# The first attention unit's operands in three parts, two of them copied inside SBUF

## Chip, cores and metric

The kernel runs on one core of one Trainium2 chip. The metric is the device time of one execution in microseconds (us); a kernel's time is the median of its runs. The engines are TensorE (PE, with its weight loads listed as PEld), VectorE (DVE), ScalarE (ACT), GpSimd (POOL) and SyncE (SP). In this kernel SyncE issues every DMA.

## What is computed

The input x has 8 sequences of 1024 tokens with 256 channels. Three sublayers follow one another: half a feed-forward step, attention with relative positions (16 heads of 16 channels), and the same half feed-forward step again.

```python
x = x + 0.5 * tanh(layernorm(x) @ W1 @ W2 @ W3 + bias)
...
xn = layernorm(x) * ln_g + ln_b
q, k, v = xn @ Wq + bq, xn @ Wk + bk, xn @ Wv + bv        # 16 heads of 16
p = sinusoidal_pe(1024, 256) @ Wp
content = einsum('bihd,bjhd->bhij', q + u_bias, k)
pos = relative_shift(einsum('bihd,jhd->bhij', q + v_bias, p))
attn = softmax((content + pos) / 4)
x = x + einsum('bhij,bjhd->bihd', attn, v) @ Wo + bo
...
x = x + 0.5 * tanh(layernorm(x) @ W1 @ W2 @ W3 + bias)
```

## The kernel before

**Two stages.** In the first, the tokens go through in 8 tiles, I = 7 down to 0, each with 128 token positions of all 8 sequences. For each tile the kernel makes the first feed-forward step, the normalisation, and the projections to queries, keys and values. Values in 16-bit floats are held as a high and a low part (`hl` 0 and 1). The results leave for tensors in device memory: `k_d`, `qv_d` (queries in eight windows of 18 positions per tile), `c_d` (a bias row per key), `v_d` and `x1c_d`.

The second stage is attention. It is cut into 64 units: 16 heads times 4 groups of query positions (`rg`). A unit has 16 steps (`step(T)`), so there are 1024 steps. A step computes two score banks of 128 x 512 (`score_ops`), the row maxima (`block_max`, `row_max`), subtracts them and takes the exponential into `eT` (`soften`). After 16 steps `emit_av` multiplies `eT` by the values in `vt`.

**The order of the work** is written out by hand: each engine runs its instructions in the order of the program, and waits come from which buffers an instruction reads and writes. A buffer of a pool that is opened where an older pool lay waits for everything that used the old buffer there.

**The pass loop.** The loop at L660 runs I from 6 to -1. A pass makes the feed-forward step of tile I and the projections of tile I+1; the value products of tile I+2 (`value`, `late`) run at its start. Before its middle it stores V of tile I+2 (`store_v`, L685) and x1 of tile I+1 (`store_x1`, L686: eight additions on POOL, then one DMA). After the projections, `key_bias` (L716) makes the bias rows `cs`, and `store_qk` (L717) sends out keys, queries and bias rows of tile I+1: one DVE copy (`next_rows`) and ten DMAs. So the last pass, I = -1, projects tile 0 and stores V of tile 1 and x1 of tile 0 on the way. After the loop come the loads of the first unit (L721), the value products of tile 0 and its V store (L724).

**A unit's operands.** `UnitSet` holds them: `k` (keys, 8 chunks of the sequence, with bias rows at partitions 48, 49, 112 and 113), `qc` and `q` (queries in two layouts) and `pg` (positions). Two sets alternate. `load_q` loads queries from `qv_d` to a raw buffer (4 DMAs), `prep` yields 16 copies from the raw buffer into `qc` and `q`, and `load_k` loads keys and bias rows (6 DMAs). All three take all 8 chunks at once. For unit 0 the 16 copies are spread over POOL, DVE and ACT (L1064, L1065). A chunk is what one tile of the first stage makes: chunk i of `k` is tile i.

**Buffers around the seam.** `cvst[0]` and `cvst[1]` hold the projected queries of even and odd tiles and are the first buffers of pool `kp` (9,216 bytes per partition each); `kp` has 25,920 bytes. Behind it lies `pA`, with two buffers each of `xTb` (8,192), `cs` (2,048), `ks` (8,192) and `vs` (8,192). After `es.close()` (L860) the attention's pools lie there: `m2` (16,352 bytes: `many16`, `m0`, `m1`, `dg` and others) and behind it `ep` with the second raw buffer (4,608), `vt` (8,192) and `eT` (65,536).

Of the kernel before, what the change touches and what calls it, by code (L numbers as in the profile page):

```python
# [16 lines left out]
P = 128  # L17
NB = 8
# [4 lines left out]
NI = S // P  # L23
# [3 lines left out]
NW = 8  # L27
QP = 18
NTILE = 64 * H
MS = 16.0  # L30
UT = 16
# [11 lines left out]
def macaron_kernel(  # L43
# [23 lines left out]
    nc = tc.nc  # L67
# [8 lines left out]
    c_d = dram("c_d", (H, 2, NI, NB * P), F16)  # L76
# [50 lines left out]
    class UnitSet:  # L127
# [21 lines left out]
                w = 16 * (hl.stop - hl.start)  # L149
                yield slice(64 * n + p0, 64 * n + p0 + w), hl  # L150

        def load_q(self, u):
            rg, h = units[u]
            w = NB * QP * rg
            return [
                (
                    raws[u % 2][pr],
                    qv_d[h, hl].rearrange("t d i (e c) -> (t d) (i e) c", e=2)
                    [:, :, w : w + NB * QP],
                )  # L160
                for n in range(2) for pr, hl in self.rows(n, True)
            ]

        def prep(self, u):


            ops = []
            for n in range(2):
                pr = slice(64 * n, 64 * n + 48)
                raw = raws[u % 2][pr]  # L170
                src = raw.rearrange("p k (b t) -> p b t k", t=QP)
                for q in range(4):
                    ops.append(
                        (self.qc[pr, :, q, 16 * n : 16 * n + 16], src[:, 4 * n + q, 0:UT])
                    )
                src = raw.rearrange("p (k e) (b t) -> p e t k b", e=2, t=QP)[:, 1 - n]
                dst = self.q[pr].rearrange("p t (k b) e -> p e t k b", b=NB)[:, 1 - n]
                for t in (slice(0, 4), slice(4, 8), slice(8, 12), slice(12, 17)):
                    ops.append((dst[:, t], src[:, t]))
            return ops  # L180

        def load_p(self, u):
# [6 lines left out]
                for n in range(2) for pr, hl in self.rows(n, False)  # L189
            ]  # L190

        def load_k(self, u):
            rg, h = units[u]
            return [
                (
                    self.k[pr].rearrange("p i q r -> p i (q r)"),
                    k_d[h, hl].rearrange("t d i c -> (t d) i c")
                    [:, :, 4 * P * n : 4 * P * n + 4 * P],
                )
                for n in range(2) for pr, hl in self.rows(n, False)  # L200
            ] + [
                (
                    self.k[64 * n + 48 : 64 * n + 50].rearrange("p i q r -> p i (q r)"),
                    c_d[h, :, :, 4 * P * n : 4 * P * n + 4 * P],
                )
                for n in range(2)
            ]

    def load_all(pairs):
        for pair in pairs:  # L210
            nc.sync.dma_start(*pair)
# [4 lines left out]
    sets = [UnitSet(hp0, 0), UnitSet(hp1, 1)]  # L216
# [4 lines left out]
    raws = [raw(hp0, 0)]  # L221

    def copy16(dst, src):
        nc.gpsimd.tensor_scalar(dst, src, 1.0, 0.0, ALU.mult, ALU.add)  # L224
# [4 lines left out]
    if True:  # L229
# [5 lines left out]
        cvst = [  # L235
            kp.tile([P, 2, 2, NW, NB, QP], F16, tag=f"cv{i}", name=f"cv{i}") for i in range(2)
        ]
# [143 lines left out]
        def store_x1(I, xt):  # L381
            for b in range(NB):
                nc.gpsimd.tensor_tensor(xt[:, b, :], xt[:, b, :], cvec, ALU.add)
            nc.sync.dma_start(
                x1c_d[:, I * P : (I + 1) * P, :].rearrange("b p c -> p b c"), xt
            )
# [45 lines left out]
        def key_bias(ks, cs):  # L432


            ps = pst.tile([P, 512], F32, tag="t", name="kb")
            n = 0
            for m in range(2):
                for a, c in ((0, 0), (1, 0), (0, 1)):
                    for h in range(2):
                        mm(  # L440
                            ps[32 * h : 32 * h + 32], uv16[:, a, m, :],
                            ks[:, m, c, 4 * h : 4 * h + 4].rearrange("p b n -> p (b n)"),
                            start=n == 0, stop=n == 5, tile_position=(0, 32 * h),
                        )
                    n += 1
            nc.scalar.copy(cs[:, 0], ps[0:64])
            nc.vector.tensor_tensor(cs[:, 1], ps[0:64], cs[:, 0], ALU.subtract)
# [27 lines left out]
        def next_rows(I):  # L475
# [4 lines left out]
            else:  # L480
                nc.vector.memset(cv[:, :, NW - 1, :, 16], 0.0)

        def store_qk(I, cs, ks):
            next_rows(I)
            cv = cvst[I % 2]
            for m in range(2):
                for hl in range(2):
                    for dst, src in (
                        (k_d, ks[:, m, hl].rearrange("p b n -> p (b n)")),
                        (qv_d, cv[:, m, hl].rearrange("p w b n -> p (w b n)")),  # L490
                    ):
                        nc.sync.dma_start(dst[8 * m : 8 * m + 8, hl, :, I], src)
            for h in range(2):
                nc.sync.dma_start(
                    c_d[:, :, I, 512 * h : 512 * h + 512], cs[32 * h : 32 * h + H]
                )

        def store_v(I, vs):
            nc.sync.dma_start(
                v_d[:, :, I, :].rearrange("h p n -> p h n"),  # L500
                vs.rearrange("p h d b -> p h (d b)"),
            )
# [6 lines left out]
        xts = {NI - 1: load_x(NI - 1)}  # L509
# [149 lines left out]
        late = None  # L659
        for I in range(NI - 2, -2, -1):  # L660
            if I >= 0:
                xT, xt, so, sb = new_xT("a"), xts[I], sb, Stats("b", xts[I])
            if I >= 1:
                sa = Stats("a", xts[I - 1])
            for n in range(4):
                if late:
                    value(late[1], late[2], 2 * n)
                if I >= 0:
                    tr_group(xn, xT, n // 2, n % 2)
                if I >= 1:  # L670
                    sa.rows(2 * n, 2 * n + 2)
                if I == NI - 2 and n == 0:
                    so.again()
                if I == NI - 2 and n == 1:
                    so.both()
                    xm = so.apply("xm")
                    low(*los[2])
                    low(*los[3])
                    wes.close()
                    pA = es.enter_context(tc.tile_pool(name="pA", bufs=2))  # L680
                if n >= 2 and I >= 0:
                    ffn(xT, xt, n - 2)
                    sb.rows(2 * n - 4, 2 * n - 2)
            if late:
                store_v(late[0], late[2])  # L685
            store_x1(I + 1, xts.pop(I + 1))  # L686
            if I >= 2:
                xts[I - 2] = load_x(I - 2)
            if I >= 1:
                sa.ends()  # L690
                xn = sa.apply("xn")
            xTb = new_xT("b")
            for n in range(4):
                tr_group(xm, xTb, n // 2, n % 2)
                if n < 2 and I >= 0:
                    ffn(xT, xt, n + 2)
                    sb.rows(2 * n + 4, 2 * n + 6)
            cs = pA.tile([64, 2, 512], F16, tag="cs", name="cs")
            ks = pA.tile([P, 2, 2, NB, P], F16, tag="ks", name="ks")
            for n in range(4):  # L700
                q = query(xTb, cvst[(I + 1) % 2], n % 2, n // 2)
                k = key(xTb, ks, n % 2, n // 2)
                q()
                k()
                if I >= 0 and n == 0:
                    sb.ends()
                if I >= 0 and n == 1:
                    sb.again()
                if I >= 0 and n == 2:
                    sb.both()  # L710
                    xm = sb.apply("xm")
            if I == NI - 3:
                sets[0].clear()
            if I == NI - 4:
                sets[1].clear()
            key_bias(ks, cs)  # L716
            store_qk(I + 1, cs, ks)  # L717
            if I == 2:
                load_all(sets[0].load_p(0))
            late = (I + 1, xTb, pA.tile([P, H, DH, NB], F32, tag="vs", name="vs"))  # L720
    load_all(sets[0].load_q(0) + sets[0].load_k(0))  # L721
    for n in range(4):
        value(late[1], late[2], 2 * n)
    store_v(late[0], late[2])  # L724
# [336 lines left out]
                        pending.extend(post_ops(rg, b, m2, 1, psm, "r", {}))  # L1061

    nc.gpsimd.memset(vt[:, :, DH:, :], 1.0)
    for n, pair in enumerate(sets[0].prep(0)):  # L1064
        (copy16, nc.vector.tensor_copy, nc.scalar.copy)[n % 3](*pair)  # L1065
    load_all(load_v(0))
    for T in range(-2, NTILE - UT + 2):
        step(T)
# [51 lines left out]
    for n in range(4):  # L1120
        src = num[0][:, 2 * n : 2 * n + 2]
# [46 lines left out]
    def head(b):  # L1168
# [8 lines left out]
    ops = {  # L1177
        b: [f for f, _ in post_ops(rg, b, t3, NB, pm, "r", {"ps": ps[b], "xr": xr[:, b]})]
        for b in range(NB)
    }  # L1180
# [52 lines left out]
```

## Time and profile before

| what | us |
|---|---|
| median of 3 runs | 3067.61 (3058.85, 3067.61, 3070.53) |
| profiled execution | 3070.87 |
| its span, first to last instruction | 3069.2 |
| first stage, until TensorE's last value product ends | 282.55 |
| first score matmul | 302.02 |
| first maximum of a score bank (L933, DVE) | 303.14 |
| first exponential (L962, ACT) | 307.13 |

The page gives busy time by engine, the span in 40 slices, the chain of work that ended last, and groups of instructions by line. In a list in order of time, a row has the start, the duration, the engine, the source line, the operation, what it writes and reads with its shape, and how often it stands there in a row; in brackets is how long the engine was idle before it and what ended that. SPq is SyncE's queue: its rows are issues of DMAs, whose data land later. A row of a stretch gives the stretch, its length, the busy time and number of instructions of PE, PEld, DVE, ACT and POOL, the granted TensorE clock (1.00 is full speed), the share of the DMA engines' time and the GB/s moved.

### The profile page before, as it was taken

To read this page: it belongs to the slowest core of one execution; us is meant where nothing else is said; L and a number is where in the kernel's file an instruction comes from. 1 tells how busy PE (TensorE), PEld (TensorE's weight loads), DVE (VectorE), ACT (ScalarE), POOL (GpSimd) and SP (SyncE) were. 2 spreads that over 40 slices of the span, in tenths; PEclk is the share of its full clock that TensorE was granted. 3 is DMA by queue.
4 is the path that set the end of the run, shared out by engine and by line. 5 is a ranking of instruction groups with operands and counts; after the bars stand their busy time and mean duration, and the time that the engine had idled before them with its cause. 6 is when DMAs were issued, how large, how long until landed. Compare 5 with 4: busy or idle time off the path is not lost.

```text
span 3069.2 us, 157389 instructions
## 1 busy us (share of the span) xinstructions
PE 2939.8 (96%) x71212; PEld 2430.2 (79%) x71212; DVE 2264.0 (74%) x5001; ACT 1668.9 (54%) x3551; POOL 1000.7 (33%) x1498
## 2 busy tenths in 40 slices
PE   7997999999999999999999999999999999999986
PEld 4655888888888888888888888888888888888875
DVE  6885777777777877777777777787777787777766
ACT  3655555555555555555555555555555555555543
POOL 8873322222221332332221332332222333242204
PEclk8998999999999999999999999999999999999998
DMA  4556222222222322322222322322222232322222
GB/s 142 186 165 181 61 68 67 65 64 61 63 64 75 83 80 82 84 70 65 63 63 76 81 78 80 80 71 68 66 66 71 81 84 79 82 61 68 68 76 78
DMA packets 333397, 250.63 MB, mean 82 GB/s; under 512 B 118885, under 2 KB 317142, under 8 KB 332246
## 3 DMA queue, kind: packets, MB, share of 16 engines
q1 hardware_dynamic: 332726, 240.56, 28.1%
q8 instruction: 558, 9.14, 1.3%
q14 instruction: 113, 0.93, 0.1%
HBM read 177.44 MB, written 62.78 MB: 78 GB/s over the span
## 4 chain that ended last, share of the span: by engine, by line
PE 80%; DVE 5%; ACT 4%; DMA 2%; issue 1%; SPq 1%; POOL 0%; ACTq 0%; POOLq 0%; DVEq 0%
PE s L1029 20%; PE s L1042 15%; PE av L970 15%; PE s L958 14%; PE s L1038 6%; PE mps L944 5%; DVE m L933 2%; ACT eT L962 2%; ACT dg L951 1%; PE pff L785 1%; ACT avs L977 1%; PE wops L785 1%; DVE m L939 1%; DMA xr<-x1c_d 1%; DVE xr L846 1%
## 5 line engine op out<-in xcount | busy, mean ns | idle before, releaser
L962 ACT ACTIVATE eT<-s 128x512 f32<-128x512 f32 x2048 | 1111.7, 594 | 1102.1 <-PE s L958 1101.4
L933 DVE TENSOR_REDUCE m<-s 128x128 f32<-128x512 f32 x2048 | 1406.1, 687 | 178.4 <-PE s L1029 37.2
L224 POOL TENSOR_SCALAR qc<-raw 48x256 f16<-48x256 f16 x507 | 330.9, 663 | 1304.1 <-PE s L1042 1266.0
L946 DVE TENSOR_REDUCE nm<-mps 128x1 f32<-128x128 f32 x1024 | 295.9, 289 | 481.7 <-ACT eT L962 471.1
L958 PE MATMUL s<-dg,many 128*128 128x512 f16 x2048 | 609.3, 378 | 43.2 <-ACT dg L951 43.2
L1029 PE MATMUL s<-qc,k 114*128 114x32 f16 x16384 | 565.1, 176 | 22.8 <-DMA k<-c_d 19.5
L1038 PEld LDWEIGHTS <-k 114*128 114x128 f16 x8192 | 354.7, 96 | 245.1 <-issue 2.2
L1029 PEld LDWEIGHTS <-k 114*128 114x128 f16 x16384 | 488.2, 96 | 24.5 <-issue 23.2
L1042 PE MATMUL s<-q,pg 112*128 112x64 f16 (+3 forms) x12288 | 482.5, 184 | 1.6 <-issue 1.6
L1029 PE MATMUL s<-q,pg 112*128 112x64 f16 (+3 forms) x12288 | 482.3, 184 | 0.1
L970 PE MATMUL av<-eT,vt 128*32 128x256 f32 x8192 | 459.8, 382 | 5.8 <-DMA vt<-v_d 5.3
L951 ACT ACTIVATE dg<-ident,nm 128x128 f16<-128x128 f16 x1024 | 413.8, 404 | 78.7 <-DVE nm L946 69.2
L970 PEld LDWEIGHTS av<-eT,vt 128*32 128x32 f32 x8192 | 317.4, 139 | 121.7 <-issue 8.9
L1042 PEld LDWEIGHTS <-pg 112*128 112x128 f16 x12288 | 407.1, 97 | 1.7 <-issue 1.7
L1029 PEld LDWEIGHTS <-pg 112*128 112x128 f16 x12288 | 407.3, 97 | 0.2 <-issue 0.2
L1042 PEld LDWEIGHTS <-k 114*128 114x128 f16 x8192 | 394.8, 101 | 12.1
L1042 PE MATMUL s<-qc,k 114*128 114x32 f16 x8192 | 365.0, 177 | 0.0
L1038 PE MATMUL s<-qc,k 114*128 114x32 f16 x8192 | 364.1, 177 | 0.0
L939 DVE TENSOR_TENSOR m<-m,m 128x128 f32<-128x128 f32 x1024 | 331.8, 324 | 35.1
L224 POOL TENSOR_SCALAR q<-raw 48x256 f16<-48x256 f16 x507 | 347.2, 696 | 20.1
L944 PE MATMUL mps<-ident,m 128*128 128x128 f32 x1024 | 317.5, 310 | 7.5 <-DVE m L939 7.5
L958 PEld LDWEIGHTS <-many 128*128 128x128 f16 x2048 | 131.8, 96 | 76.4 <-issue 76.0
(173 smaller groups left out, 1811.6 us busy)
## 6 DMA issues: line engine op xcount, KB each, us to landing
k<-k_d SPq DMA_DIRECT2D x128, 256.0 KB
vt<-v_d SPq DMA_DIRECT2D x128, 256.0 KB
raw<-qv_d SPq DMA_DIRECT2D x128, 144.0 KB
pg<-g_d SPq DMA_DIRECT2D x128, 132.5 KB
k<-k_d SPq DMA_DIRECT2D x128, 128.0 KB
h_d<-avs SPq DMA_DIRECT2D x126, 128.0 KB
qv_d<-cv SPq DMA_DIRECT2D x32, 288.0 KB
raw<-qv_d SPq DMA_DIRECT2D x128, 72.0 KB
```

Source lines behind the costliest of these rows:

```text
L224: nc.gpsimd.tensor_scalar(dst, src, 1.0, 0.0, ALU.mult, ALU.add)
L933: nc.vector.tensor_reduce(n, s_t[T][c].rearrange("p (j c) -> p c j", c=P), AX.X, ALU.max)
L939: nc.vector.tensor_tensor(n, n, m_t[T], ALU.max)
L944: nc.tensor.transpose(ps, m_t.pop(T), ident)
L946: r = nc.vector.tensor_reduce(nm, ps, AX.X, ALU.max, negate=True)
L951: nc.scalar.activation(dg, ident16, AF.Copy, scale=nm)
L958: mm(ps, many16, bass.AP(dg.tensor, dg.offset, [list(dg.ap[0]), [0, 4], [1, P]]), start=False, stop=True, skip_group_check=True,)
L962: nc.scalar.activation(eT[:, 4 * c : 4 * c + 4, :, t, :], ps.rearrange("p (j b n) -> p j b n", j=4, b=NB), AF.Exp,)
L970: mm(av[32 * c : 32 * c + 32, q, :], vt[:, j, :, 4 * q + c], eT[:, j, 4 * q + c].rearrange("p t n -> p (t n)"), start=j == 0, stop=j == NI ...
L1029: f()
L1038: f()
L1042: f()
```

## The change

The first unit's operands come in three parts now. Chunks 2 to 7 are loaded from device memory in pass I = 0, as soon as tile 2 has been stored. Chunks 1 and 0 never take that way: `first_unit` copies them from the tiles in SBUF that the projections wrote (`ks`, `cvst`, `cs`), 16 DMAs a chunk, after `key_bias` and ahead of `store_qk`. The 16 copies of `prep` become two sets: chunks 2 to 7 on POOL alone, in pass 0, and chunks 0 and 1 on POOL and DVE by turns, in pass -1. In the last pass the stores of x1 of tile 0 and V of tile 1 stand behind `store_qk`, x1 first. The loads and copies that stood behind the loop are gone. The stores to `k_d`, `qv_d` and `c_d` all stay, since later units read them.

```diff
-        def load_q(self, u):
+        def load_q(self, u, lo=0):
...
-                    raws[u % 2][pr],
+                    raws[u % 2][pr, 2 * lo :],
                     qv_d[h, hl].rearrange("t d i (e c) -> (t d) (i e) c", e=2)
-                    [:, :, w : w + NB * QP],
+                    [:, 2 * lo :, w : w + NB * QP],
...
-        def prep(self, u):
+        def prep(self, u, lo=0, hi=NI):
...
+            ks = slice(lo, hi)
...
-                    ops.append(
-                        (self.qc[pr, :, q, 16 * n : 16 * n + 16], src[:, 4 * n + q, 0:UT])
-                    )
+                    ops.append((
+                        self.qc[pr, :, q, 16 * n + 2 * lo : 16 * n + 2 * hi],
+                        src[:, 4 * n + q, 0:UT, 2 * lo : 2 * hi],
+                    ))
...
-                    ops.append((dst[:, t], src[:, t]))
+                    ops.append((dst[:, t, ks], src[:, t, ks]))
...
+        def first_unit(I, cs, ks):
+
+            us = sets[0]
+            for n in range(2):
+                for g, hl in enumerate((0, 0, 1)):
+                    p = 64 * n + 16 * g
+                    nc.sync.dma_start(
+                        us.k[p : p + 16, I].rearrange("p q r -> p (q r)"),
+                        ks[0:16, 0, hl, 4 * n : 4 * n + 4].rearrange("p b n -> p (b n)"),
+                    )
+                for g, hl in enumerate((0, 1, 0)):
+                    p = 64 * n + 16 * g
+                    nc.sync.dma_start(
+                        raws[0][p : p + 16, 2 * I : 2 * I + 2],
+                        cvst[I % 2][0:16, 0, hl, 0 : NW : 4]
+                        .rearrange("p w b n -> p w (b n)"),
+                    )
+            for n in range(2):
+                for hl in range(2):
+                    p = 64 * n + 48 + hl
+                    nc.sync.dma_start(
+                        us.k[p : p + 1, I].rearrange("p q r -> p (q r)"),
+                        cs[32 * n : 32 * n + 1, hl],
+                    )
...
-            if late:
-                store_v(late[0], late[2])
-            store_x1(I + 1, xts.pop(I + 1))
+            if I == 0:
+                load_all(sets[0].load_q(0, 2) + sets[0].load_k(0, 2))
+            if I >= 0:
+                if late:
+                    store_v(late[0], late[2])
+                store_x1(I + 1, xts.pop(I + 1))
...
             key_bias(ks, cs)
+            if I <= 0:
+                first_unit(I + 1, cs, ks)
+            if I == 0:
+                for pair in sets[0].prep(0, 2):
+                    copy16(*pair)
+            if I < 0:
+                for n, pair in enumerate(sets[0].prep(0, 0, 2)):
+                    (copy16, nc.vector.tensor_copy)[n % 2](*pair)
             store_qk(I + 1, cs, ks)
+            if I < 0:
+                store_x1(I + 1, xts.pop(I + 1))
+                store_v(late[0], late[2])
...
-    load_all(sets[0].load_q(0) + sets[0].load_k(0))
     for n in range(4):
         value(late[1], late[2], 2 * n)
     store_v(late[0], late[2])
...
     nc.gpsimd.memset(vt[:, :, DH:, :], 1.0)
-    for n, pair in enumerate(sets[0].prep(0)):
-        (copy16, nc.vector.tensor_copy, nc.scalar.copy)[n % 3](*pair)
     load_all(load_v(0))
```

`load_k` takes `lo` in the same way as `load_q`; `NW` is 8 and `NI` is 8.

More of the change, by code (lines that the diff above doesn't have):

```diff
@@ L190, in load_p, with load_k @@
             ]
-        def load_k(self, u):
+        def load_k(self, u, lo=0):
             rg, h = units[u]
@@ L195, in load_k @@
                 (
-                    self.k[pr].rearrange("p i q r -> p i (q r)"),
+                    self.k[pr, lo:].rearrange("p i q r -> p i (q r)"),
                     k_d[h, hl].rearrange("t d i c -> (t d) i c")
-                    [:, :, 4 * P * n : 4 * P * n + 4 * P],
+                    [:, lo:, 4 * P * n : 4 * P * n + 4 * P],
                 )
@@ L202, in load_k @@
                 (
-                    self.k[64 * n + 48 : 64 * n + 50].rearrange("p i q r -> p i (q r)"),
-                    c_d[h, :, :, 4 * P * n : 4 * P * n + 4 * P],
+                    self.k[64 * n + 48 : 64 * n + 50, lo:].rearrange("p i q r -> p i (q r)"),
+                    c_d[h, :, lo:, 4 * P * n : 4 * P * n + 4 * P],
                 )
```

## The prediction

> **What bounds the kernel now.** I read the page first, then the time-ordered list of all engines around the seam between the projections and the first scores, then SyncE's own queue, then busy time and DMA rate by stretch.
>
> ```profile
> span 3069.2 us, 157389 instructions
> PE 2939.8 (96%) x71212; PEld 2430.2 (79%) x71212; DVE 2264.0 (74%) x5001; ACT 1668.9 (54%) x3551; POOL 1000.7 (33%) x1498
> ```
>
> TensorE is busy for 96% of the span, and the steady score loop (400 to 440 us: PE busy 39.79 of 40) isn't touched. What can be won lies in TensorE's idle time at the seam. The time-ordered list there:
>
> ```profile
> 277.14 5.41 PE L466 MATMUL vv<-v,xTb 128*128 128x256 f16 x48
> ...
> 292.41 0.17 DVE L872 MEMSET many<- 128x128 f16 x1 [13.72 <-DMA qv_d<-cv]
> ...
> 302.02 0.59 PE L1029 MATMUL s<-qc,k 114*128 114x32 f16 x16 [19.47 <-DMA k<-c_d]
> ...
> 303.14 0.69 DVE L933 TENSOR_REDUCE m<-s 128x128 f32<-128x512 f32 x1 [5.52 <-PE s L1029]
> ...
> 307.13 1.08 ACT L962 ACTIVATE eT<-s 128x512 f32<-128x512 f32 x2 [0.70 <-DMA vt<-v_d]
> ```
>
> TensorE ends the last value product at 282.55 and starts the first score at 302.02: a hole of 19.5 us, which the last key load ends. That is 0.63% of the time and the ceiling of any gain. But the list shows two further gates: DVE's `many16` waits 13.72 us for the last `qv_d` store, and the first exponential (`eT`) stands behind a DMA of `v_d`. What SyncE does in the hole:
>
> ```profile
> 273.36 1.51 SPq L492 DMA_DIRECT2D k_d<-ks  x1
> 278.71 0.62 SPq L492 DMA_DIRECT2D qv_d<-cv  x1
> ...
> 285.28 1.37 SPq L492 DMA_DIRECT2D qv_d<-cv  x1
> 286.76 3.27 SPq L494 DMA_DIRECT2D c_d<-cs  x2
> 290.12 2.61 SPq L211 DMA_DIRECT2D raw<-qv_d  x4
> 292.77 2.54 SPq L211 DMA_DIRECT2D k<-k_d  x4
> 295.36 1.32 SPq L211 DMA_DIRECT2D k<-c_d  x2
> 296.78 0.36 SPq L499 DMA_DIRECT2D v_d<-vs  x1
> 297.26 6.41 SPq L211 DMA_DIRECT2D raw<-qv_d  x4
> 304.76 1.30 SPq L211 DMA_DIRECT2D vt<-v_d  x2
> ```
>
> Stores of tile 0 until 290.03, ten loads until 296.68, 5.0 us more until the last lands, then the last store of V. It has landed when SyncE gets past its wait for it, at 304.7. The rates by stretch (PE clock, DMA share, GB/s at the end of the line):
>
> ```profile
> 263.00:271.00 8.00, 7.87 (x44) 4.20 (x43) 5.76 (x16) 5.91 (x11) 1.79 (x3) 1.00 0.55 200
> 272.00:278.00 6.00, 5.76 (x35) 2.59 (x34) 4.01 (x13) 3.04 (x7) 0.00 (x0) 1.00 1.03 320
> ```
>
> A q/k store set (2.3 MB) goes out at 200 GB/s, 11.5 us of SyncE; V and x1 stores drain at 320 GB/s.
>
> **Who owns the memory.** From the tile shapes: the buffers of the score loop are laid on those of the projections. `m2` begins where `cvst[0]` lay (9,216 B: `many16`, `m0`, `m1`, `dg`), so DVE's first maximum must wait for tile 0's `qv_d` stores. `eT` (65,536 B) begins 29,152 B behind that start and covers `ks`, `cs` and both `vs`, so the first exponential must wait until the V stores of tiles 1 and 0 have landed. The change doesn't move these owners.
>
> **The change, part by part**, along SyncE's queue.
>
> Tile 2..7 loads (L153, L192), moved to the pass I=0: ten issues as at 290.12 to 296.68, 6.5 us. Today SyncE idles between x1's store (ends 246.2) and 253.55, so they cover 242.96 to 249.5; V(2) and x1(1) follow to 252.7. These 2.1 MB now start behind 0.92 MB of loads and drain until about 258, not 251. Nothing waits for them but SyncE itself, which in this program keeps at most eight DMAs unfinished; so the eighth copy of tile 1 goes at about 258.
>
> Sixteen copies per tile from SBUF to SBUF. The nearest row is the tail's copies of 16 partitions by 1 KB:
>
> ```profile
> L1140 SPq DMA_DIRECT2D tn<-avs x8: 534/588/1662, 3018.1 to 3026.2; - x8
> ```
>
> Lower end 0.534 us an issue, upper 1.662; I take the median 0.588, since size and kind are the same: 9.4 us a set. They land about 1.4 us after issue there (second `td<-inv` ends near 28.1, POOL starts at 3029.49). Tile 1's: seven before 258, nine more to 263.4. Its q/k store set, until now ending at 270.17, follows for 11.9 us to 275.3. Tile 0's copies: all data ready by 278.55 (`cs`, L447), so SyncE alone paces them, 275.3 to 284.7. Its store set: to 296.6. Then x1(0), V(1) and V(0), which the change puts behind it.
>
> The Trainium skill speaks against such copies: "DMA: Bandwidth & Descriptors", section "Measured (HBM→SBUF, 128 partitions, SWDGE, issued from GpSimd)", tells to batch to 1 MiB and says that under 64 KB descriptors dominate. By its section on the anatomy of one DMA, about 2.0 us fixed each, 32 copies one after the other would be an estimated 64 us and the kernel far slower; the tail's rows show four in 2.43 us instead, one behind the other without waiting, so I go by the rows.
>
> Copies on POOL and DVE. prep(0,2): 16 on POOL at 6/8 of 0.66 us (L224 rows), 8 us, from 259.3 (after `xm`) to about 268, while POOL has nothing until the x1 additions, which are moved. Without that cover they would cost those 8 us. prep(0,0,2): 8 each on POOL and DVE, of a quarter size; bounds 0.1 to 0.66 us, taken 0.2 to 0.25, nearest by size: done 1.3 us after the last raw lands, about 285, with one to four us more at the upper end. On DVE the wait for raw holds `next_rows`, so the first `qv_d` store, which SyncE reaches at 285.3 only. The x1 additions (8 x 0.69 = 5.5 us) then end at 291, before SyncE comes to that store at 296.6. The copies removed from ACT, DVE and POOL at L1065 (294.2 to 299) lay beside the key loads: nothing.
>
> So the scores can start at about 286.5, sixteen us earlier. What is late next:
>
> 1. `m0`: last `qv_d` issue ends near 293.2; today 286.65 to 292.41 is 5.8 us of landing; so 299.0 against 303.14. TensorE runs ahead by under two score tiles and stops at the first row maximum (L944).
> 2. `eT`: three 1.05 MB stores at 320 GB/s are 9.8 us. They begin about 1.8 us behind the last `c_d` issue (270.17 to 272, when the rate rises), so 298.4, and V(0) has landed near 308.3, against the first exponential at 307.13 today.
>
> Third, the granted clock: 0.58 over the hole and 0.55 in 302 to 306. Today the slow stretch is filled with scores alone (first tile 1.84 us, later 1.7). After the change TensorE will have idled again until 308 and meet its slow stretch in full steps with the 512-column products of L958 (376 ns, at most 757): plus 0.7 us.
>
> Sum against the profiled run's 3070.87 us (1.67 around the span): +1.2 for `eT`, -0.1 (TensorE one row maximum further), +0.7, so about +2 us: 3072.7. The three runs have a median of 3067.61, so by them 3069.5.
>
> **The rivals.**
>
> A. V's stores land sooner than I think (other engines already free, 340 GB/s), and `m0` decides. Then the maximum starts 4.1 us earlier and the exponential with it: with the clock about -3.5, 3064. For it: only half the DMA engines' time is used in the q/k stores (0.55). Against: V(0) is last of three.
>
> B. The reuse waits don't bind, and the hole closes as the change says: 302.02 to 286.5 is -15.5 us, 3052; at the best -19.5, 3048. For it: the wait in the list that ends the hole is a key load. Against: DVE's 13.72 us for `qv_d`, and the stores moved behind the copies.
>
> C. Slower: SyncE's copies cost more than 0.588 us. Each tenth of a us moves V(0) by 32 x 0.1 = 3.2 us at most. Slower by 0.5% (15.3 us) needs 13 us more, so 1.0 us a copy; at 1.662 it would be 34 us, 3103. For it: the first of the tail's copies, and `qv_d` issues of 1.37 when the queue is full. Against: the other seven. At about 1.05 this gives 3085.
>
> D. The copies aren't in time and the seam is as before, within 3 us: in my case anyway.
>
> **Chances.** My case with D 0.62, A 0.20, B 0.06, C 0.12. What a measurement of this kernel tells from no change is about 0.5%, 15 us; the three runs alone lie 11.7 us apart. A and my own case are "same"; of B about two thirds would be faster beyond it, of C about nine tenths slower. So faster 0.05, same 0.84, slower 0.11. The predicted time is my case, 3069.5; the range reaches down through A and the spread of the runs to 3054, and up to the point where C begins, 3084.
>
> **What would show it.** Right: TensorE's first score at 285 to 288; DVE's `many16` at 297 to 301; the first exponential at 305 to 311, released by a V store; SyncE's copies 0.53 to 0.65 us each; TensorE idle twice between 288 and 308; the loop after it unchanged. Wrong: the exponential running at 302 or before (A), or at 290 (B); copies near 1 us (C); or a `tp`, `qq` or `kk` product in 245 to 282 that waits for SyncE's queue.

## The result and the profile after

| | us |
|---|---|
| kernel before, median of 6 runs | 3064.35 (3058.85 to 3070.53) |
| changed kernel, median of 6 runs | 3075.18 (3072.93 to 3076.76) |
| ratio, with its 95% interval | 1.0039 [1.0028, 1.0049] |
| profiled execution of the changed kernel | 3076.16 |

The changed kernel is slower by some 11 us, 0.4%. That is within the 0.5% that the prediction called no change, though the interval lies clear of 1. A second series of 12 runs of the same kernel, on another occasion, gave 3072.29 against 3066.03, 1.0024 [1.0013, 1.0035]: 6 us.

The busy times of the page are nearly those of before:

```profile
span 3074.4 us, 157451 instructions
PE 2935.3 (95%) x71212; PEld 2428.6 (79%) x71212; DVE 2260.7 (74%) x5004; ACT 1665.3 (54%) x3546; POOL 1005.5 (33%) x1516
```

TensorE has 4.5 us less busy time in a span that is 5.2 us longer: the loss is idle time. The time-ordered list of TensorE, DVE and ScalarE at the seam (start, duration, engine, line, operation, what it writes and reads; in brackets the idle time before it and what ended that):

```profile
283.33 0.59 PE L1069 MATMUL s<-qc,k 114*128 114x32 f16 x16 [7.66 <-DMA k<-cs]
...
296.68 0.17 DVE L912 MEMSET many<- 128x128 f16 x1 [14.91 <-DMA qv_d<-cv]
...
296.76 1.22 DVE L973 TENSOR_REDUCE m<-s 128x128 f32<-128x512 f32 x2
...
298.36 0.47 PE L984 MATMUL mps<-ident,m 128*128 128x128 f32 x1 [11.85 <-DVE m L979]
...
299.25 0.40 ACT L991 ACTIVATE dg<-ident,nm 128x128 f16<-128x128 f16 x1 [22.46 <-DMA x1c_d<-xt]
...
307.82 1.09 ACT L1002 ACTIVATE eT<-s 128x512 f32<-128x512 f32 x2 [8.18 <-DMA v_d<-vs]
308.47 0.59 PE L1069 MATMUL s<-qc,k 114*128 114x32 f16 x16 [6.01 <-ACT eT L1002]
```

The single hole of 19.5 us before the first score has become three holes in a row. TensorE now starts scoring 7.7 us behind the last value product (275.67), released by the last of the copied bias rows. It stops soon after, 11.85 us, for the first row maximum, which DVE couldn't begin until tile 0's `qv_d` stores were done. And ScalarE, which has built `dg` by 299.65, idles another 8.18 us: the exponential waits for a store of V. TensorE's third hole, 6.01 us, ends with that exponential.

Because the first stage of the two profiled executions differs by 6.9 us for a reason that was also met without the change (last section), the seam is counted from the end of tile 0's last value product in all that follows:

| us behind the last value product | first score | first maximum | first exponential | exponential no. 200, counted from 0 |
|---|---|---|---|---|
| before (product ends at 282.56) | 19.46 | 20.58 | 24.57 | 274.13 |
| before, taken again (273.88) | 18.44 | 19.56 | 24.16 | 274.00 |
| changed (275.67) | 7.66 | 21.09 | 32.15 | 282.47 |
| changed, taken again (272.84) | 7.84 | 21.36 | 32.10 | 283.21 |

The score starts 10.6 to 11.8 us sooner and the exponential 7.6 to 8.0 us later. By exponential no. 200 the loss is 8.5 to 9.2 us against the second profile of before, and it is never won back: between the first profiles of the two kernels it is 8.3 at no. 200 and at no. 540, 12.3 at no. 550 (unit 17 has begun) and 11.8 at no. 2000. Where an experiment below is set against before's seam, the second profile of before is meant. SyncE's queue shows how it got there:

```profile
245.07 3.69 SPq L491 DMA_DIRECT2D k<-ks  x3
...
255.09 2.48 SPq L505 DMA_DIRECT2D k<-cs  x4
257.61 0.67 SPq L519 DMA_DIRECT2D k_d<-ks  x1
...
269.88 3.19 SPq L491 DMA_DIRECT2D k<-ks  x3
...
279.19 2.48 SPq L505 DMA_DIRECT2D k<-cs  x4
281.71 0.66 SPq L519 DMA_DIRECT2D k_d<-ks  x1
...
289.83 1.39 SPq L519 DMA_DIRECT2D qv_d<-cv  x1
291.27 2.78 SPq L521 DMA_DIRECT2D c_d<-cs  x2
294.15 0.52 SPq L386 DMA_DIRECT2D x1c_d<-xt  x1
294.72 5.28 SPq L526 DMA_DIRECT2D v_d<-vs  x2
```

From 245 to 300 the queue is never empty: copies of tile 1, its store set, copies of tile 0 (269.88 to 281.67: 11.8 us for 16), its store set, x1, and only then both V stores, whose landing the exponential waits for.

The profile also has a loss far from the edit. At the start of unit 17 TensorE stands still, and no semaphore is behind it. Changed kernel, TensorE in order of time:

```profile
985.28 0.22 PE L1069 MATMUL s<-q,pg 112*128 112x64 f16 x2
987.88 0.43 PE L1069 MATMUL s<-q,pg 112*128 112x64 f16 x10 [2.38 <-issue]
988.24 8.79 PE L1010 MATMUL av<-eT,vt 128*32 128x256 f32 x128
```

And the same place in the kernel before, taken again:

```profile
975.42 0.44 PE L1029 MATMUL s<-q,pg 112*128 112x64 f16 x11 [0.21 <-issue]
975.79 7.14 PE L970 MATMUL av<-eT,vt 128*32 128x256 f32 x128
```

Here 2.38 - 0.21 and 8.79 - 7.14 make 3.8 us. So, like for like, 8.5 at the seam and 3.8 here are 12.3 us. The spans, each less its first stage, differ by 5.2 + 6.9 = 12.1 against the first profile of before and by 13.5 - 1.8 = 11.7 against the second. Whether the pause at unit 17 belongs to the change isn't shown; both profiles of the changed kernel have it, neither of before's has.

### The profile page after: what moved, and what is told of

Same layout as the page of the kernel before. It is cut to its first block, busy times and chain, and to the rows that moved or that the text cites. A ratio compares the mean times of both kernels' runs of the same rounds, so it can differ in the third digit from the quotient of the medians.

```text
span 3074.4 us, 157451 instructions
## 1 busy us (share of the span) xinstructions
PE 2935.3 (95%) x71212; PEld 2428.6 (79%) x71212; DVE 2260.7 (74%) x5004; ACT 1665.3 (54%) x3546; POOL 1005.5 (33%) x1516
## 4 chain that ended last, share of the span: by engine, by line
PE 82%; DVE 7%; ACT 5%; DMA 2%; issue 2%; SPq 1%; POOL 1%; ACTq 0%; POOLq 0%; DVEq 0%
PE s L1069 20%; PE s L1082 15%; PE av L1010 15%; PE s L998 14%; PE s L1078 6%; PE mps L984 5%; DVE m L973 2%; ACT eT L1002 2%; ACT dg L991 1%; PE vv L468 1%; PE pff L825 1%; ACT avs L1017 1%; PE qq L455 1%; PE wops L825 1%; PE kk L455 1%
## 5 line engine op out<-in xcount | busy, mean ns | idle before, releaser
L226 POOL TENSOR_SCALAR qc<-raw 48x256 f16<-48x256 f16 (+2 forms) x516 | 332.8, 655 | 1324.5 <-PE s L1082 1265.4
L1082 PEld LDWEIGHTS <-k 114*128 114x128 f16 x8192 | 394.7, 101 | 12.2
L226 POOL TENSOR_SCALAR q<-raw 48x256 f16<-48x256 f16 (+3 forms) x516 | 350.3, 690 | 20.4
```

Of the source, the lines that this page charges most:

```text
L1082: f()
```

## The experiments

The theory: the first exponential is held by the V stores, because `eT` lies on the `vs` buffers and SyncE reaches these stores late; behind that gate stands a second one, the first maximum, held by `qv_d` stores because `m2` lies on `cvst`. Rivals: the copies themselves, whatever the order; the first maximum alone; the earlier loads.

**The kernel before again**, for the scatter.

> The kernel before, unchanged, profiled a second time. In its first profile a DVE copy of tile 3's pass (the next_rows copy) took 5.04 us and the first stage ended at 282.55 us; in the changed kernel's profile the same copy took 0.49 us and the stage ended at 275.68. If that is run-to-run scatter, this profile ends the first stage near 275.7 at least as often as near 282.5, the time from the last value product to the first exponential is again 24.6 us (24 to 25.2), and the ratio is 1.000 within 0.003. If it is of the program, the copy takes 5 us again and the stage ends at 282.5.

3068.36 against 3062.45, 1.0011 [0.9997, 1.0026]: no difference clear of noise, though these medians of one and the same kernel lie 5.9 us apart. A difference of some us between medians is therefore weak evidence by itself; what an experiment does at the seam is read from its profile. Its seam agrees with the first profile's within 1.1 us at each point, while its first stage is 8.7 us shorter.

**The V and x1 stores back at their old place** in the last pass; all else as changed.

```diff
-            if I >= 0:
-                if late:
-                    store_v(late[0], late[2])
-                store_x1(I + 1, xts.pop(I + 1))
+            if late:
+                store_v(late[0], late[2])
+            store_x1(I + 1, xts.pop(I + 1))
...
             store_qk(I + 1, cs, ks)
-            if I < 0:
-                store_x1(I + 1, xts.pop(I + 1))
-                store_v(late[0], late[2])
```

> The changed kernel, but x1 of tile 0 and V of tile 1 are stored at the start of the last pass again, as in the kernel before. Theory (SyncE's queue is full from tile 2's stores on, V of tile 0 is the last of three megabyte stores behind it, and the first exponential waits for it): two of the three stores now drain while SyncE issues the small copies, so the first exponential comes 4 to 6 us earlier, at 302 to 304 (307.82 in the changed kernel's profile), although the first score comes 2 to 3 us later, at 285 to 286.5; the time falls by 4 to 6 us. Rival (the copies' landing or the pause of TensorE sets the loss): the exponential follows the first score and comes 2 to 3 us later, and the time rises by as much. Rival (scatter): no change.

The list of DVE and ScalarE:

```profile
299.98 0.17 DVE L908 MEMSET many<- 128x128 f16 x1 [14.71 <-DMA qv_d<-cv]
...
304.25 1.08 ACT L998 ACTIVATE eT<-s 128x512 f32<-128x512 f32 x2 [1.30 <-PE s L994]
```

The exponential no longer waits for V, and yet it comes 30.9 us behind the value products, only 1.3 earlier than in the changed kernel. The two V/x1 stores now stand ahead of the copies and push tile 0's store set back, so that the first maximum comes at 26.7 instead of 21.1. One gate was taken away and the other closed later. 3073.62, 1.0028 [1.0012, 1.0043]. The hoped-for 4 to 6 us were a miss: the order of the queue alone can't mend this.

**`eT` on memory that V doesn't use.** The raw buffer and `vt` in a pool of their own, then `t1`, and `eT` behind that.

```diff
-    ep = pool("ep", 1, se)
-    raws.append(raw(ep, 1))
+    ev = pool("ev", 1)
+    raws.append(raw(ev, 1))
...
-    vt = ep.tile([P, NI, 32, NB], F32, tag="vt", name="vt")
+    vt = ev.tile([P, NI, 32, NB], F32, tag="vt", name="vt")
+    ev.tile([P, 256], F32, tag="pad", name="pad")
+    t1 = pool("t1", 1)
+    ep = pool("ep", 1, se)
...
-    t1 = pool("t1", 1, side="right")
```

> The changed kernel with eT at another place, where ks, cs and vs did not lie (the tail's buffers of pool t1 are opened ahead of eT on the left side); the order of all work stays. eT now covers the buffer of x1 of tile 0, whose store is issued at 294.2. Theory: the first exponential no longer waits for V of tile 0 but follows the first row maximum, which DVE starts at 296.7: exponential at 300.5 to 302, time 6 to 7 us less than the changed kernel's 3075.18. Rival (a landing of copies, GpSimd's and DVE's small copies, or the clock sets the loss): the exponential stays at 307 to 308.5 and the time too.

```profile
305.90 0.40 ACT L994 ACTIVATE dg<-ident,nm 128x128 f16<-128x128 f16 x1 [22.54 <-DVE nm L989]
...
307.65 1.08 ACT L1005 ACTIVATE eT<-s 128x512 f32<-128x512 f32 x2 [1.35 <-PE s L1001]
```

The wait for `v_d` is gone and the exponential comes 25.4 us behind the value products (282.25), 6.7 earlier than in the changed kernel with an unchanged queue. It now follows the chain of the first maximum. So the V gate was what held it, and the maximum alone would have held it at about 25, hardly later than before's 24.2. 3070.1, 1.0016 [1.0002, 1.0030].

**Without the copies.** `first_unit` and the second `prep` are left out, so unit 0's chunks 0 and 1 aren't filled; the order of the stores stays as changed.

```diff
-            if I <= 0:
-                first_unit(I + 1, cs, ks)
...
-            if I < 0:
-                for n, pair in enumerate(sets[0].prep(0, 0, 2)):
-                    (copy16, nc.vector.tensor_copy)[n % 2](*pair)
```

> The changed kernel without the 32 copies inside SBUF and without the 16 small copies from raw of chunks 0 and 1: the first unit's keys and queries of chunks 0 and 1 are left out (zero). Theory: one set's SyncE time (11.8 us) goes off the queue ahead of V of tile 0, the other set's turns into waiting for data; the first exponential comes 10 to 13 us earlier, at 295 to 298. Rival (the three stores drain at their own pace whatever stands ahead of them): 307 to 308 as now.

```profile
289.91 0.17 DVE L907 MEMSET many<- 128x128 f16 x1 [13.80 <-DMA qv_d<-cv]
...
301.05 1.08 ACT L997 ACTIVATE eT<-s 128x512 f32<-128x512 f32 x2 [8.17 <-DMA v_d<-vs]
```

Both gates are still there, with waits about as long as in the changed kernel, but everything stands 11.1 us earlier: the exponential at 21.07 behind the value products (279.98). 11.1 us is about what one set of 16 copies holds SyncE (11.8). So the set of tile 1 (12.5 us in the changed kernel) costs next to nothing: without the copies SyncE stands idle for 14.2 us between 249.4 and 276.1, until keys and queries of the two tiles are ready, and a set has room there. 3067.57, 0.9999 [0.9984, 1.0013].

**The changed kernel again** gave 1.0024 [1.0013, 1.0035].

> The changed kernel, unchanged, profiled a second time, in one session with the three that follow. The seam, counted from the end of tile 0's value products, repeats if it is of the program: first score 7.7 us behind it, first exponential 32.1 (31 to 33), while the end of the first stage itself may lie anywhere from 273 to 283 us, as it did for the kernel before (282.6 and 273.9). Ratio 1.002 to 1.005.

Its seam is that of the first profile within 0.4 us until the first maxima and 0.7 us later at exponential no. 200. The pause at unit 17 is there too, 4.8 us.

**Both gates away**: the old place of the stores, `eT` apart, and a gap of 9,216 bytes ahead of `m2`, so that it doesn't lie on `cvst[0]`.

```diff
+    gap = pool("gap", 1)
+    gap.tile([P, 2304], F32, tag="gap", name="gap")
```

> stores_first with both groups of buffers moved: m2 (many16, m0, m1, dg) begins behind cvst[0], and eT lies behind the tail's buffers of t1. Theory: two gates stood one behind the other, V of tile 0 (eT) and tile 0's qv_d stores (m0); stores_first ended at the second. With both gone the first maximum follows the first score by 1.1 us and the exponential the maximum by 4.0, as in the kernel before: first score 13.2 us behind the value products as in stores_first, exponential at 18 to 19.5 (30.9 in stores_first, 24.2 and 24.6 in the kernel before); the time 4 to 7 us below the kernel before. Rival (the pause of TensorE and its clock, or POOL's and DVE's copies, set the loss): exponential at 30 as in stores_first.

```profile
284.10 0.17 DVE L910 MEMSET many<- 128x128 f16 x1
...
286.21 0.69 DVE L973 TENSOR_REDUCE m<-s 128x128 f32<-128x512 f32 x1 [1.95 <-PE s L1069]
```

`many16` waits for no store now, and the first maximum waits for TensorE's score. The exponential comes at 18.15, as expected, 6.0 us earlier than before. 3059.74 against 3066.03, 0.9981 [0.9969, 0.9992]. So the early operands do pay at the seam, once nothing waits for the end of their queue. How much of it lasts is less clear. In the profiled execution 2.2 of the 6.0 us are left at the 33rd exponential, and its span less the first stage is that of before within 0.1 us; the gain of 6.3 us in the median isn't traced to the seam by it.

**The store sets of tiles 1 and 0 behind both sets of copies**, on top of that, to bring the last copies forward.

```diff
-            store_qk(I + 1, cs, ks)
+            next_rows(I + 1)
+            if I == 0:
+                held = (I + 1, cs, ks)
+            else:
+                if I < 0:
+                    store_qk(*held)
+                store_qk(I + 1, cs, ks)
```

(`prep` of chunks 2 to 7 moves to the last pass, behind the x1 store.)

> all_apart, with tile 1's q/k stores held back behind tile 0's copies, and GpSimd's 16 larger copies behind its x1 additions. Theory (what is left is SyncE's queue ahead of tile 0's copies): the copies then go as their data come, the first score 1 to 3 us behind the value products, the exponential at 6 to 9; but unit 1's raw loads and key loads move behind 20 stores and land near 33 and 40, where its scores are due at about 35, so 4 to 9 us are given back at the 15th or 16th step: time 8 to 14 us below the kernel before. Rival (copies land late whatever the queue): first score stays at 13.

The first score starts 1.1 us behind the value products, but the exponential comes at 19.1, not at the expected 6 to 9. The table of waits of this run, from 275 to 330 (us in total, times, longest):

```profile
DVE many L915 <- DMA qv_d<-cv: 15.2, 1, 15.2
```

With the gap, `m2` starts on `cvst[1]`, tile 1's queries. As long as tile 1's stores ended early this was free; now they are late. I had overlooked a third owner. 3059.13, 0.9980 [0.9969, 0.9991].

**The store sets in halves**: first unit 1's share of both tiles, then its loads, then the rest. Unit 1's raw queries go to the first raw buffer here, and unit 2's query loads overwrite part of them before all of them are copied.

```diff
+                both = (held, (I + 1, cs, ks))
+                for ms, bias in (((0,), False), ((), True), ((1,), False)):
+                    for tile_ in both:
+                        store_qk(*tile_, ms, bias)
+                    if bias:
+                        load_all(sets[1].load_q(1))
```

> stores_behind, with the stores ordered by need: heads 0 to 7 of tiles 1 and 0, the bias rows, unit 1's query loads (into the first raw buffer), then heads 8 to 15, then V. Theory: first score and exponential as in stores_behind (1 to 3 and 6 to 9 us behind the value products), the wait at unit 1 shrinks to 0 to 4 us: 12 to 18 us below the kernel before. Rival: the stall at unit 1 is set by the key loads, which still stand behind all stores, and stays at 4 to 9 us.

A miss for the same reason: `cvst[1]`'s last store is now still later. `many16` comes at 26.6, the exponential at 30.96. 3076.93, 1.0043 [1.0026, 1.0059], over six runs. Again the first maximum is paced by the last store of the buffer under it.

**The early loads alone**, without the copies: chunks 2 to 7 are loaded in pass I = 0 as in the change, the stores stay where they were before, and chunks 0 and 1 are loaded behind the loop as before.

```diff
+            if I == 0:
+                load_all(sets[0].load_q(0, 2) + sets[0].load_k(0, 2))
...
-    load_all(sets[0].load_q(0) + sets[0].load_k(0))
+    load_all(sets[0].load_q(0, 0, 2) + sets[0].load_k(0, 0, 2))
```

> One part of the change alone: chunks 2 to 7 of the first unit are loaded in pass 0 and copied by GpSimd there; chunks 0 and 1 are loaded from device memory behind the last stores, where the kernel before loads all eight, and nothing is copied inside SBUF. The stores of x1 and V stand where the kernel before has them. Theory (the 32 copies and the two moved megabyte stores lose the time, the early loads alone win a little): still ten issues behind the last store, but a quarter of the bytes, so the last lands 2 to 3 us after its issue and not 5.0: first score 16 to 18 us behind the value products (19.5 and 18.4 in the kernel before), exponential at 21 to 23 (24.6, 24.2); time 1 to 4 us below the kernel before. Rival (the moved loads and POOL's copies themselves disturb the passes): exponential later than 24.6, or the first stage longer by some us.

SyncE's queue and, in a second fence, DVE:

```profile
279.61 1.94 SPq L213 DMA_DIRECT2D raw<-qv_d  x4
281.59 2.05 SPq L213 DMA_DIRECT2D k<-k_d  x4
283.69 1.11 SPq L213 DMA_DIRECT2D k<-c_d  x2
284.91 0.39 SPq L526 DMA_DIRECT2D v_d<-vs  x1
```

```profile
287.38 0.69 DVE L965 TENSOR_REDUCE m<-s 128x128 f32<-128x512 f32 x1 [3.49 <-PE s L1061]
```

The ten loads of two chunks are issued in 5.2 us and land sooner. First score at 14.2, exponential at 19.2: 5.0 us earlier than before, somewhat more than expected. 3060.11 against 3065.36, 0.9987 [0.9976, 0.9999]; the profiled run also has pauses without a wait of 5.4 us at unit 17 and 3.4 at unit 33, and less its first stage it is 4.0 us longer than before. So at the seam the first of the three parts of the change gains, and the copies with the moved stores turn that into a loss; for the whole time this rests on the median, whose interval only just excludes 1.

**All gates away**: the store sets behind the copies, and a gap of 18,432 bytes, past both `cvst` buffers (the tail's `xr8` moves to the other side to make room).

```diff
-    gap.tile([P, 2304], F32, tag="gap", name="gap")
+    gap.tile([P, 4608], F32, tag="gap", name="gap")
```

> stores_behind with m2 behind both cvst buffers (there it lay on cvst[1], whose stores that order makes late, and DVE's first memset came 14.8 us behind the value products); xr8 of the tail goes to the right side to make room. Theory: no gate of reused memory is left, so the maximum follows the first score and the exponential comes 6 to 8 us behind the value products; unit 1's loads stay where they are, landing near 33 and 40 for scores due at 35, so 4 to 9 us are given back there: time 8 to 13 us below the kernel before, 2 to 6 below all_apart. Rival: another gate (vt or the raw buffer lie on cs and ks now) holds POOL and the gain is as in all_apart, 5 to 7 us.

DVE, and in a second fence TensorE:

```profile
273.06 0.17 DVE L915 MEMSET many<- 128x128 f16 x1
...
275.50 1.42 DVE L978 TENSOR_REDUCE m<-s 128x128 f32<-128x512 f32 x2 [2.27 <-PE s L1074]
```

```profile
274.59 0.55 PE L1074 MATMUL s<-qc,k 114*128 114x32 f16 x16 [1.37 <-DMA k<-cs]
...
287.70 0.37 PE L1074 MATMUL s<-qc,k 114*128 114x32 f16 x8 [1.22 <-issue]
...
294.45 0.43 PE L1074 MATMUL s<-q,pg 112*128 112x64 f16 x10 [2.24 <-issue]
...
306.55 0.33 PE L989 MATMUL mps<-ident,m 128*128 128x128 f32 x1 [1.72 <-issue]
...
316.59 0.55 PE L1074 MATMUL s<-qc,k 114*128 114x32 f16 x16 [1.77 <-DMA pg<-g_d]
```

The hole is closed: score at 1.4, exponential at 5.96, 18.2 us earlier than before. But by the 33rd exponential only 7.5 of it is left. Part goes in three pauses without a wait while the held-back stores drain, 5.2 us, and part in unit 1's loads, which come late. 3055.98, 0.9971 [0.9958, 0.9983], which is 8.9 us of 3065.36 and within what was expected.

**DVE's copy of the next rows on ScalarE** (it had taken 5 us in the first profile), once on the kernel above and once on the kernel before.

```diff
-            nc.vector.tensor_copy(cv[:, :, NW - 1, :, 16], nxt[:, :, 0, :, 0])
+            nc.scalar.copy(cv[:, :, NW - 1, :, 16], nxt[:, :, 0, :, 0])
```

> all_clear with the next_rows copy (128 x 32) on ScalarE. In three of ten profiles that copy of tile 3 took 5.0 to 5.3 us on DVE, ending when POOL's additions ended; the others took 0.22 to 0.52. If DVE waits for POOL there, the first stage ends at 272 to 274 us in every run and the runs scatter less; the median falls by 0 to 4 us against all_clear. Rival (the long copy is a sign of something else): the stage end scatters as before.

> The kernel before with the next_rows copy on ScalarE and nothing else. Same theory as for all_clear_act: first stage ends at 272 to 275 us, median 1 to 5 us below the kernel before. Rival: no change.

On the kernel above: 3055.25, 0.9966 [0.9953, 0.9979], the lowest median of all. On the kernel before: 3061.66, 0.9990 [0.9979, 1.0002], not clear of no change, though its copy took 0.33 us every time. The runs were to scatter less; they still lie 11.5 us apart on the kernel above (14.4 without this edit) and 11.1 on the kernel before. The two `all_clear` versions beat both kernels; between them the intervals overlap.

## Why the prediction was right, and where it was off

**The gates: right.** The prediction said that the key loads end the hole in the list but don't decide, that `m2` lies on `cvst[0]` and `eT` on `vs`, and that the V stores would be last. The first score came at 290.2 on the time base of before's profile (283.33 + 6.88, the difference of the first stages), the forecast was 286.5 and the span given for it 285 to 288; the order is right, the place 3.7 us off. The wait of the first exponential is named `v_d<-vs`; taking `eT` off that memory removed it and 6.7 us. That the time, 3075.18, lies inside the range of 3054 to 3084 is owed to the width of the range, which follows the scatter of the runs, and not to the sum: the sum said +2, and the medians of the first series differ by 10.8.

**The size: the terms of SyncE's queue were too small.** The sum had +1.2 us for `eT`; measured were 7.6 (against the first profile of before) to 8.0. On before's time base:

| end of | predicted | measured | the step is off by |
|---|---|---|---|
| tile 1's copies | 263.4 | 264.45 | +1.05 |
| tile 1's store set | 275.3 | 276.7 | +0.3 (12.2 us, not 11.9) |
| tile 0's copies | 284.7 | 288.55 | +2.5 (11.9 with the gap ahead of them, not 9.4) |
| tile 0's store set | 296.6 | 300.9 | +0.5 |
| V(0) landed, exponential | 308.3 | 314.7 | +2.1 |

The copies are 1.05 + 2.5 of it, but not because a copy is dearer than I thought. The median issue took 0.60 us in the first set and 0.59 in the second, and the sum had 0.588. What failed is the step from one issue to a set: the first three issues of a set, behind loads and stores, took 3.69 and 3.19 us together, and the other thirteen 0.65 to 0.67 each with the gaps between them. A set so held SyncE for 12.5 and 11.8 us, not 9.4. The tail of before had shown it already:

```profile
3018.14 3.61 SPq L1140 DMA_DIRECT2D tn<-avs  x4
3021.85 2.43 SPq L1143 DMA_DIRECT2D td<-inv  x4
3024.38 2.43 SPq L1140 DMA_DIRECT2D tn<-avs  x4
3026.91 2.44 SPq L1143 DMA_DIRECT2D td<-inv  x4
```

These sixteen copies took 11.2 us, 0.70 each. The row that I used is a median over L1140 alone, and leaves out the slow start and the gaps.

The store sets add 0.8. The last row is the drain of the three stores: they moved 320 GB/s from 295.8 to 301.8, as forecast, but 255 from 301.8 to 307.6, where the sum kept 320. Unit 1's loads were issued from 300.1 on; whether they slow the last store, no run tells. Together this is 6.4 us, and 1.2 + 6.4 = 7.6. So two of the signs I had named, `many16` at 297 to 301 (303.6 on this base) and the exponential at 305 to 311, were overshot. The third, copies of 0.53 to 0.65 us, came true for 26 of the 32 and was no sign of a sum that holds.

**The clock: near.** +0.7 was predicted for waking in a slow stretch. Within the first five steps the offset grew by 0.5 against the second profile of before (7.99 to 8.5) and by 0.8 against the first (7.6 to 8.3). The granted clock was 0.50 from 308 to 312 here and 0.55 from 302 to 306 in before; that it makes the growth wasn't tested. The 757 ns given for the longest product of L958 stand in no row: the longest took 634 in both kernels.

**Unseen: unit 17.** 3.8 to 4.8 us in the profiled runs have no term in the sum at all. It contradicts the sign "the loop after it unchanged". With the 6.4 it makes the gap from +2 to the 12 by which the profiled executions differ, less their first stages. The medians differ by 11 in the first series and 6 in the second.

**The rivals.** A (the maximum decides) fell: V landed last. But `eT_apart` shows what A would have been, 25.4 us behind the value products, hence no gain and not the 3.5 us I gave it, for the maximum came at 303.6, not at the 299.0 of the forecast. B (nothing binds) fell in the changed kernel; as a price of the closed hole its -15.5 to -19.5 was also too good: `all_clear` closes it, and keeps 7.5 of 18.2. C (SyncE's copies cost more) named part of the error, but a set came to 0.74 to 0.78 us a copy, not to 1.0, and the surplus lay mostly at the start of the set. The Trainium skill's fixed 2.0 us a DMA ("DMA: Bandwidth & Descriptors", the anatomy of one DMA), which the page gives for DMAs issued by GpSimd, would have made an estimated 64 us of the 32 copies one after the other. No run agrees: the two sets, issued by SyncE, took 24.3 us of it, and leaving them out moved the exponential by 11.1.

**What stays open.** Why the pause at unit 17 comes in some executions. The profile shows an instruction load of 16 KB there, and doesn't say for which engine. In the seven profiles with the pause (the changed kernel twice, stores first, no copies, stores behind, early loads, `all_clear_act`) this load begins between 0.6 us ahead of the pause's place and 1.0 behind it, and TensorE goes on 2.5 to 3.0 us after the load's start. In the other seven (before twice, `eT` apart, both gates away, halves, `all_clear`, before with ScalarE's copy) it begins 3.1 to 3.6 us ahead, and there is no such pause. So a late load goes with the pause every time; no run tells what makes it late, and no experiment moved it alone.

## What to carry over

When a wait is removed, list every buffer that the next instructions write, and who last used the memory under it: here three owners stood one behind the other, and each removal only showed the next. A transfer that is brought forward in a full in-order queue pushes back all that stands behind it; its price is the queue time of what passes it (16 copies, 11 to 12 us), to be paid by whoever waits for the last store. The memory map was the cheaper lever: with the pools laid apart and the stores put back ahead, a loss of 6 to 11 us in the median became a gain of 6 to 10. And price a row of small transfers by a whole row of them: the median of single issues was right within 0.02 us, and the set still took a quarter to a third longer.

## What the runs showed of the hardware

**A small DVE copy that ends with GpSimd's additions.** The first stage of the profiled runs ended anywhere from 272.0 to 282.6 us. In before's first profile, DVE in order of time and then POOL:

```profile
199.88 5.04 DVE L479 COPY cv<-cv 128x32 f16<-128x32 f16 x1
```

```profile
199.31 5.52 POOL L383 TENSOR_TENSOR xt<-xt,cvec 128x256 f32<-128x256 f32 x8
```

The copy of 32 elements a partition takes 0.22 to 0.52 us elsewhere. In three profiles it started while the first of POOL's eight additions ran, and each time it ended within 0.1 us of the last of them: 5.04 us here, 5.11 in `eT` apart and 5.33 without the copies. The first stage ends between 280.0 and 282.6 in these three and between 272.0 and 275.7 in the rest. On ScalarE it took 0.33 us each time and the stage ended at 272.2 and 273.1. A stage longer by some 7 us could account for part of the 11.7 us between the first three runs of before, but not for all the scatter: with the copy on ScalarE the twelve runs of before still lie 11.1 us apart. The Trainium skill, "SBUF — State Buffer", section "Who interferes with whom", speaks of an exclusive lock on ports that the two engines share, held for one instruction; here the copy stood through some seven of them.

**Pauses without a semaphore.** TensorE lost 1.9 to 5.4 us at the start of unit 17 in seven of fourteen profiles, each by a pause that the profile puts down to no wait ("issue"), with an instruction load beside it, 700 us behind the seam. Two versions can so differ by microseconds in a place that the edit doesn't touch.

**A queue of small copies.** 16 copies from SBUF to SBUF of at most 16 partitions took 11.8 us of SyncE: 3.19 for the first three, behind a store set, and 0.65 each for the others, gaps included. The median issue was 0.59, as in the tail, where 16 copies took 11.2.
